# Value projection of a two-layer transformer by seven products of blocks in units of two token tiles

## The chip, the cores and the metric

The kernel runs on one core of one Trainium2 chip. A core has a matrix engine (TensorE, PE in the profile, with its weight loads as PEld), a vector engine (VectorE, DVE), a scalar engine (ScalarE, ACT), GpSimd (POOL) and SyncE (SP), whose queue issues this kernel's DMA transfers. The metric is the device time of one execution in microseconds (us); less is better. All data are float32.

## The reference

Two layers, each with attention and a feed-forward part side by side on the same normalised input, for 2 batches of 1024 tokens of 512 features and 16 heads of 32. Layer 0 has 2048 hidden units, layer 1 has 1408, ternary weights and scales.

```python
x = L0_attn_X                                   # (2, 1024, 512)
xn = _layernorm(x)
x = x + _L0_attn_ref(xn, Wq, Wk, Wv, Wo) + _L0_ffn_ref(xn, w_gate, w_up, w_down)
xn = _layernorm(x)
x = x + _L1_attn_ref(xn, ...) + _L1_ffn_ref(xn, ...)

# attention, both layers, up to the kind of rope
Q = X @ Wq.T; K = X @ Wk.T; V = X @ Wv.T
Qr, Kr = _rope(heads of Q), _rope(heads of K)
scores = einsum('bhqd,bhkd->bhqk', Qr, Kr) * DH ** (-0.5)       # causal
heads = einsum('bhqk,bhkd->bqhd', softmax(scores), heads of V)
return heads @ Wo.T

# feed-forward, layer 0 (layer 1: the same with scales on gate, up and down)
return einsum('bsh,dh->bsd', silu(x @ w_gate.T) * (x @ w_up.T), w_down)
```

The change concerns `V = X @ Wv.T`: 1024 tokens by 512 features in, 512 features out, once for each layer and batch.

## The kernel before

**Phases and steps.** A phase is one layer and batch; there are four, run one after the other. In each phase the heads go in four groups of four; in a group the queries go in four blocks of 256, and a step is one query block against 256 keys. A group has 10 steps, a phase 40, and `t0` is a phase's first step. A step issues scores (`sc`), scales them, masks the last of a block, takes maxima (`rmax`, `mtr`, which come back by DMA as `mb`), subtracts them, takes exponentials, sums these on GpSimd (`acc`) and, five steps after the scores (LAG = 5), multiplies them with the values on TensorE (`av`). So the first values of a phase, those of token tiles 0 and 1, are read at step t0 + 5, tiles 2 and 3 at t0 + 7, 4 and 5 from t0 + 10.

**What fills TensorE.** Beside attention's own matmuls, the class `Fill` hands TensorE the other work, a share in each step that spreads what is left evenly over the steps left in the phase. Its lists are: `main` (units of the hidden layer and what stands between phases: transposes, first projections), `downs` (rows of the down projection), `outs` (rows of the output projection), `qk` (units of queries and keys that are to be taken into main from a given step on) and, before the change, `values`. `choose` takes the next one by what its operands are waiting for; when the next main item isn't ready or is held, only downs and outs may pass it.

**Units.** The hidden layer's gate and up projections, and the queries and keys of groups 1 to 3, were already computed by seven products of 2x2 blocks (the Winograd form of Strassen's scheme): a `Unit` has four items, `first`, `second`, `third` and `fourth`, with two, two, two and one products, two PSUM banks held through it (`x` and `y`), copies of banks by ScalarE (`keep`), and sums of weight blocks that GpSimd makes while the unit before is in its third (`nxt.sums()`) and fourth item (`nxt.more_sums()`). The sums of the input blocks are made once a phase (`xs`, `ln_sums`, `ln_last_sum`). `decide`, called after each second item, puts the next unit of `qk` into main after the running unit's fourth if its step is due. There are 53 such hidden units and 12 of queries and keys.

**Values before.** `project_v(ph, t)` (line 812) makes the values of token tiles t and t + 4 for t = 0 to 3. It multiplies the first half of the features of tile t (2 matmuls into bank `ps_v`), keeps a copy (`vv`), multiplies the difference of the two tiles' first halves (`t1`) and the second half of tile t + 4 (4 matmuls into `ps_w`), adds the copy (VectorE, tile t + 4), and finishes tile t in `ps_v` with the second half (2 matmuls, then a copy by ScalarE). These are eight products of blocks: 8 matmuls with 128 tokens as the weights and 512 output features as the moving columns for each two tiles, 32 in a phase. They are issued as items of their own of cost 8, from steps t0 + 4, 4, 5, 5 on (phase 0: from step 0), and at the latest at t0 + 4, 4, 6, 6 (`queue_phase`, line 1354), but not between a unit's second and fourth item.

**The planner.** All instructions are recorded into `Schedule`, which simulates engines with durations of its own, then sorts them anew with due times (`again`, line 340) and emits them. So any change to the work can move instructions everywhere in the program. All of them carry the recorder's line, 265, in the profile; groups are told apart by the tiles' names.

**Buffers that the change touches.** `tmp`, tag `xs`, has two buffers of one tile of 128 x 512: raw input of the layer norm, and operands of `scale_down` (line 890), which multiplies the eleven row blocks of layer 1's down weights by their scales during phase 0 and stores them for the last two phases (`wds`). `wv` has one buffer, loaded anew for each phase after the last values of the phase before.

Of the kernel before, what the change touches and what calls it, by code (L numbers as in the profile page):

```python
# [11 lines left out]
F32 = mybir.dt.float32  # L12
AF = mybir.ActivationFunctionType
ALU = mybir.AluOpType
# [4 lines left out]
P = 128  # L19
# [4 lines left out]
QC = T // P  # L24
# [16 lines left out]
def ts(n, size):  # L41
    return slice(n * size, (n + 1) * size)
# [364 lines left out]
def two_layers(ctx: ExitStack, tc: tile.TileContext, x_in, attn_w, ffn_w, ffn_s, rope, out):  # L407
# [39 lines left out]
    def bank(name, shape=(P, TB), hold=False):  # L447
        nc.advance(nc.tensor.free)
        n = min((n for n in range(3) if not bank_held[n]), key=lambda n: (bank_free(n), bank_last[n].first.seq if bank_last[n] else 0))
        bank_held[n] = hold  # L450
        t = bank_last[n] = p_m.tile(list(shape), F32, tag=f"m{n}", name=name)
        if hold:
            bank_of[name] = n
        return t

    def let_go(name):
        bank_held[bank_of.pop(name)] = False
# [131 lines left out]
        nc.sync.dma_start(out=w[:, 2:4, :], in_=src[D // 2 :, :].rearrange("(c p) e -> p c e", p=P))  # L589

    class Unit:

# [44 lines left out]
        def product(self, bank, a, b, start=False):  # L639
            for c in range(2):  # L640
# [6 lines left out]
                    skip_group_check=True,  # L647
                )

        def scale(self):  # L650

            return None

        def needs(self, kind):

            if kind == "second":
                return [self.one, self.s12]
            if kind == "third":
                return [self.u, self.p5, self.s4]
            if kind == "fourth":  # L660
                return [self.p5]
            return []

        def first(self):
            self.begin()
            a, _ = self.weights()
            x0 = xnT[self.ph, 0]
            self.x = bank(f"ux{self.name}", hold=True)
            self.product(self.x, a[:, 0:2], x0[:, 0:2], start=True)
            one = self.one = keep(self.x, f"p1{self.name}")  # L670
            z = bank(f"uz{self.name}")
            self.product(z, a[:, 2:4], x0[:, 2:4], start=True)
            self.c11(z, one)

        def second(self):
            t1, t2, _ = xs[self.ph]
            self.product(self.x, self.s12[:, 1], t2)
            self.u = keep(self.x, f"u{self.name}")
            self.y = bank(f"uy{self.name}", hold=True)
            self.product(self.y, self.s12[:, 0], t1, start=True)  # L680
            self.p5 = keep(self.y, f"p5{self.name}", self.scale())

        def third(self, nxt):
            _, b = self.weights()
            x1 = xnT[self.ph, 1]
            self.product(self.x, b[:, 0:2], x1[:, 0:2])
            if nxt:
                nxt.sums()
            if self.scale() is None:
                nc.vector.tensor_tensor(self.p5, self.x, self.p5, ALU.add)  # L690
            else:
                nc.vector.scalar_tensor_tensor(self.p5, self.x, self.scale(), self.p5, ALU.mult, ALU.add)
            self.c22(self.p5)
            self.product(self.y, self.s4, x1[:, 2:4])
            let_go(f"uy{self.name}")
            self.c12(self.y, self.u)

        def fourth(self, nxt):
            _, b = self.weights()
            self.product(self.x, b[:, 2:4], xs[self.ph][2])  # L700
            let_go(f"ux{self.name}")
            if nxt:
                nxt.more_sums()
            self.c21(self.x)

    def keep(bank, name, scale=None):
        t = t5_p.tile([P, TB], F32, tag="t5", name=name)
        if scale is None:
            nc.scalar.copy(t, bank)
        else:  # L710
            nc.scalar.activation(t, bank, AF.Copy, scale=scale)
        return t
# [50 lines left out]
    class QueriesKeys(Unit):  # L763
        def __init__(self, ph, g, opens):

            self.ph, self.g, self.name, self.opens = ph, g, f"_qk{ph}_{g}", opens
            self.kind, self.part = "qk", g
# [4 lines left out]
        def begin(self):  # L772
            pass
# [2 lines left out]
            nc.vector.tensor_tensor(one, bank, one, ALU.add)  # L776
            rotated(self.ph, self.g, "q", 0, one)

        def c22(self, k1):
            rotated(self.ph, self.g, "k", 1, k1)  # L780

        def c12(self, bank, u):
# [24 lines left out]
    def load_wv(ph):  # L807
        layer, _ = phases[ph]
        wv[ph] = wv_p.tile([P, DC, D], F32, tag="wv", name=f"wv{ph}")
        nc.sync.dma_start(out=wv[ph], in_=attn_w[layer][2].rearrange("(c p) e -> p c e", p=P))  # L810

    def project_v(ph, t):


        x0, x1, t1 = xnT[ph, 0], xnT[ph, 1], xs[ph][0]
        cols = ts(t, P)

        def product(bank, a, c0, start):
            for c in range(2):
                nc.tensor.matmul(  # L820
                    bank,
                    a[:, c, cols],
                    wv[ph][:, c0 + c, :],
                    start=(start and c == 0),
                    stop=(c == 1),
                    skip_group_check=True,
                )

        ps0 = bank(f"ps_v{ph}_{t}", hold=True)
        product(ps0, x0[:, 0:2], 0, True)  # L830
        both = keep(ps0, f"vv{ph}_{t}")
        ps1 = bank(f"ps_w{ph}_{t}")
        product(ps1, t1, 0, True)
        product(ps1, x1[:, 2:4], 2, False)
        for n in (0, 4):
            v[ph, t + n] = xp.tile([P, D], F32, tag=f"v{t + n}", name=f"v{ph}_{t + n}")
        nc.vector.tensor_tensor(v[ph, t + 4], ps1, both, ALU.add)
        product(ps0, x0[:, 2:4], 2, False)
        let_go(f"ps_v{ph}_{t}")
        nc.scalar.copy(v[ph, t], ps0)  # L840
        if t == QC // 2 - 1 and ph + 1 < len(phases):
            load_wv(ph + 1)

    parts = {}

# [98 lines left out]
    class Hidden(Unit):  # L944
# [19 lines left out]
        def c11(self, bank, one):  # L964
            nc.vector.tensor_tensor(self.h[0], bank, one, ALU.add)

        def c22(self, up):
            self.up = up

        def c12(self, bank, u):  # L970
            nc.vector.tensor_tensor(self.h[1], bank, u, ALU.add)
# [235 lines left out]
    class Fill:  # L1207
# [2 lines left out]


        def __init__(self):
            self.timed, self.main, self.downs, self.outs, self.qk, self.values = [], [], [], [], [], []

            self.later = 0.0
            self.turn = False
            self.unit = None
# [15 lines left out]
            self.main[at:at] = items  # L1233

        def left(self, end):
            n = 8.0 * len(self.values) + sum(item[0] for item in self.main) + self.later
            n += sum(len(d[2]) for d in self.downs) + 14.0 * len(self.qk)
            return n + sum(1.0 for o in self.outs if o[0] < end)

# [39 lines left out]
                    return o  # L1279
            return None  # L1280

        def do_values(self):
            self.values.pop(0)[2]()
            self.turn = False
            return 8.0

        def do_output(self, o):
            self.outs.remove(o)
            output_alone(*o[1:])
# [9 lines left out]
        def choose(self, step):  # L1299

            main = self.main[0] if self.main else None
            v = self.values[0] if self.values and self.values[0][0] <= step else None
            if main and main[2] in ("third", "fourth"):
                v = None
            if v and v[1] <= step:
                return self.do_values, 8.0
            o = self.late_output(step)
            if o and self.wait([oT[o[1], o[2], o[3] // 2]]) <= 0.0:
                return (lambda: self.do_output(o)), 1.0
            full = main and main[2] == "first" and self.downs and self.downs[0][0] <= main[4] - 2  # L1310
            one = (lambda: self.do_main(step)), main[0] if main else 0.0
            full = full or (main and main[2] == "third" and getattr(main[3], "opens", 0) > step)
            if main and not full:
                needs = main[3].needs(main[2]) if isinstance(main[3], Unit) else main[3]() if main[3] else []
                main_wait = self.wait(needs, 0 if main[2] in ("third", "fourth") else 1)
                if main_wait <= SOON or not main[0]:
                    return one
            else:
                main_wait = float("inf")
            if self.ready_down():  # L1320
                _, p, ks, t = self.downs[0]
                if self.wait([hT[p, k, t // 4] for k in ks]) < main_wait or full or not main:
                    return (lambda: self.do_down(step)), 2.0
            if v:
                return self.do_values, 8.0
            if main and not full:
                return one
            return ((lambda: self.do_output(o)), 1.0) if o else None
# [25 lines left out]
    def queue_phase(ph):  # L1354
# [7 lines left out]
            for t in range(QC):  # L1362
                fill.outs.append((t0 + g * per_group + done_at(ph, g, t), ph, g, t))
        fill.outs.sort()
        for t in range(QC // 2):

            fill.values.append((t0 + (4, 4, 5, 5)[t] if ph else 0, t0 + (4, 4, 6, 6)[t], lambda t=t: project_v(ph, t)))
        if ph == 0:
            for k in range(HIDDEN[1]):
                fill.at(t0 + 4 + k, lambda k=k: scale_down(k))  # L1370
        if nxt:
            for t in range(QC):
                fill.at(t0 + per_phase - 22 + t, lambda t=t: load_raw(nxt, t))
# [217 lines left out]
```

## Time and profile before

| what | us |
| --- | --- |
| median of three runs | 1867.2 (1863.83 to 1868.71) |
| the profiled execution: time | 1868.41 |
| the profiled execution: span from its first to its last instruction | 1866.6 |
| value matmuls `ps_v`, busy | 60.9 |
| value matmuls `ps_w`, busy | 60.3 |
| hidden units' matmuls `ux`, `uy`, `uz`, busy (7 groups of 212) | 703.2 |
| down projection `d` from `hT`, busy | 401.0 |
| ScalarE copies `vv` and `v`, 16 each | 9.2 and 9.3 |
| VectorE adds into `v`, 16 | 11.0 |

The granted TensorE clock was 0.997 on the mean of the span. A row of the groups reads: engine, operation, what is written and read, shapes, count, then busy time and mean duration (ns) of one, then the engine's idle time before these instructions and what ended it. Matmul durations include a pipeline's length and overlap from one to the next; busy time counts an overlapped stretch once. "issue" is a wait for nothing that the profile shows.

### The profile page before, as it was taken

Reading aid. Unit: us, or ns where it says so; the run is one execution under the profiler, and the core shown is the slowest. Engines: PE = TensorE matmul, PEld = TensorE weight load, DVE = VectorE, ACT = ScalarE, POOL = GpSimd, SP = SyncE. Lnnn points to the kernel's source line nnn. Section 1 sums busy time; section 2 is a strip of 40 time slices with the busy share of each in tenths; the row PEclk is TensorE's granted clock in tenths of the full one; section 3 lists DMA queues with packets and bytes.
Section 4 is the critical chain, followed back from the end, with each engine's and each line's share of the span. In section 5 each row is a group of like instructions: output and inputs, shape, how many; then the busy total and the mean of one; then the engine's idle time right before and its main releaser. Section 6 shows DMA issues by size and latency. Waiting matters only on the chain.

```text
span 1866.6 us, 25444 instructions
## 1 busy us (share of the span) xinstructions
PE 1838.2 (98%) x9180; PEld 838.8 (45%) x9180; DVE 1408.2 (75%) x1958; ACT 1038.8 (56%) x1243; POOL 1179.8 (63%) x1124
## 2 busy tenths in 40 slices
PE   7999999999999999999999999999999999999997
PEld 3444444444444444444444444444444444444443
DVE  3577866758778577587587786978879887989787
ACT  3465554546557464445375645665665665666661
POOL 5575856756567355373356875878758766766664
PEclk9999999999999999999999999999999999999998
DMA  5544222222243222222223323222222312221111
GB/s 197 161 140 140 83 65 68 85 66 83 68 136 108 94 80 63 68 79 81 68 82 102 119 85 129 64 74 73 80 83 88 124 35 91 72 69 52 57 39 67
DMA packets 139726, 164.21 MB, mean 88 GB/s; under 512 B 13264, under 2 KB 93136, under 8 KB 139600
## 3 DMA queue, kind: packets, MB, share of 16 engines
q1 hardware_dynamic: 139600, 162.58, 27.5%
q8 instruction: 73, 1.20, 0.3%
q14 instruction: 53, 0.43, 0.1%
HBM read 134.23 MB, written 28.31 MB: 87 GB/s over the span
## 4 chain that ended last, share of the span: by engine, by line
PE 88%; DVE 5%; DMA 3%; POOL 2%; ACT 1%; issue 1%; SPq 0%; POOLq 0%; DVEq 0%; ACTq 0%
PE d L265 23%; PE ux L265 18%; PE uy L265 8%; PE av L265 8%; PE sc L265 8%; PE uz L265 4%; PE ux_qk L265 4%; PE ps_w L265 3%; PE ps_v L265 3%; DVE s L265 2%; PE uy_qk L265 2%; PE ps_k L265 2%; PE ps_o L265 1%; PE ps_q L265 1%; DMA mb<-md 1%
## 5 line engine op out<-in xcount | busy, mean ns | idle before, releaser
L265 DVE TENSOR_TENSOR s<-s,mb 128x1024 f32<-128x1024 f32 (+2 forms) x448 | 492.1, 1132 | 24.7 <-DMA mb<-md 24.7
L265 POOL TENSOR_TENSOR acc<-acc,s 128x512 f32<-128x512 f32 (+1 forms) x384 | 478.1, 1270 | 39.5 <-ACT s L265 38.0
L265 ACT ACTIVATE s<-s 128x1024 f32<-128x1024 f32 (+1 forms) x320 | 305.3, 971 | 182.0 <-DVE s L265 179.7
L265 DVE TRANSPOSE_TENSOR_REDUCE rmax<-s 128x32 f32<-128x1024 f32 (+1 forms) x320 | 350.9, 1118 | 72.5 <-POOL s L265 42.1
L265 PE MATMUL d<-wd,hT 128*128 128x512 f32 x864 | 401.0, 597 | 0.4 <-ACT xnT L265 0.2
L265 ACT ACTIVATE s<-sc 128x1024 f32<-128x1024 f32 (+1 forms) x320 | 282.9, 933 | 207.9 <-PE sc L265 204.0
L265 POOL TENSOR_TENSOR acc<-s 128x512 f32<-128x512 f32 (+1 forms) x128 | 153.6, 1214 | 235.4 <-PE av L265 173.2
L265 PEld LDWEIGHTS d<-wd,hT 128*128 128x128 f32 x864 | 162.8, 191 | 201.1 <-issue 187.3
L265 DVE TENSOR_TENSOR x<-d,x 128x512 f32<-128x512 f32 x224 | 151.7, 678 | 93.1 <-PE d L265 92.1
L265 ACT ACT_TABLE_LOAD x160 | 205.3, 1283 | 10.9 <-DVE s L265 8.1
L265 PE MATMUL av<-s,v 128*32 128x256 f32 (+1 forms) x2560 | 159.7, 365 | 3.0 <-ACT s L265 2.0
L265 PEld LDWEIGHTS av<-s,v 128*32 128x32 f32 x2560 | 66.9, 109 | 148.7 <-issue 105.0
L265 POOL TENSOR_SCALAR_AFFINE_SELECT s<-s 128x512 f32<-128x512 f32 x128 | 89.9, 716 | 66.6 <-ACT s L265 64.9
L265 POOL TENSOR_TENSOR hT<-p,hT 128x512 f32<-128x512 f32 x53 | 75.8, 1430 | 75.2 <-ACT hT L265 75.2
L265 PE MATMUL ux<-xs,wu 128*128 128x512 f32 x212 | 100.8, 598 | 3.1 <-DVE p L265 3.1
L265 PE MATMUL ux<-xnT,wu 128*128 128x512 f32 x212 | 101.5, 601 | 0.0
L265 PE MATMUL ux<-xs,ws 128*128 128x512 f32 x212 | 101.0, 599 | 0.0
L265 PE MATMUL ux<-xnT,wg 128*128 128x512 f32 x212 | 101.0, 599 | 0.0
L265 PE MATMUL uy<-xnT,ws 128*128 128x512 f32 x212 | 99.7, 593 | 0.0
L265 PE MATMUL uz<-xnT,wg 128*128 128x512 f32 x212 | 99.6, 592 | 0.0
L265 PE MATMUL uy<-xs,ws 128*128 128x512 f32 x212 | 99.6, 592 | 0.0
L265 PE MATMUL d<-wo,oT 128*128 128x512 f32 x192 | 99.3, 599 | 0.1
(158 smaller groups left out, 2412.7 us busy)
## 6 DMA issues: line engine op xcount, KB each, us to landing
mb<-md SPq DMA_DIRECT2D x64, 512.0 KB, 3.7
wg<-in_gate SPq DMA_DIRECT2D x54, 256.0 KB, 2.8
wd<-in_down SPq DMA_DIRECT2D x32, 256.0 KB, 3.0
xr<-xm SPq DMA_DIRECT2D x32, 256.0 KB, 3.1
wu<-in_up SPq DMA_DIRECT2D x28, 256.0 KB, 2.9
s12gu<-ws SPq DMA_DIRECT2D x26, 256.0 KB, 2.0
ws<-s12gu SPq DMA_DIRECT2D x26, 256.0 KB, 2.6
wd<-wds SPq DMA_DIRECT2D x22, 256.0 KB, 2.9
```

What stands on the lines that cost most here:

```text
L265: target(*[get(a) for a in args], **{k: get(a) for k, a in kwargs.items()})
```

## The change

- `project_v` goes, and a class `Values(Unit)` comes: two units a phase, `pair` 0 and 1. Pair 0 makes token tiles 0, 1, 4, 5, pair 1 makes 2, 3, 6, 7. Each has seven products of blocks. A product has four matmuls (two token tiles, two blocks of 128 features) with 128 tokens as weights and 256 output features as moving columns; the two tiles' results stand side by side in one bank, 256 columns each, and only the first matmul of the bank is flagged as a start.
- Sums of blocks of `wv` are made once a phase by GpSimd, on 128 x 512 elements each: s1, s2 (in the two `xs` buffers of `tmp`), s4 (a new buffer `wv4`), and A11 - A21 in place in `wv`. Both pairs use them.
- Values are written by halves of the features for two tiles at once: three VectorE adds and one ScalarE copy a unit, besides the three copies `keep`. The value tiles are now pairs, with the same total size.
- The values' list, its item `do_values` and its two steps go. The two units stand in `qk` with steps t0 + 3 and t0 + 4, and `begins` holds their first items until t0 + 4 and t0 + 5, in phase 0 too.
- `Unit.first`, `second`, `third`, `fourth` take their blocks from `first_blocks` and `blocks`; the add that ended `third` stands in each unit's `c22`; `needs` names the sums of inputs too.
- `scale_down(k)` moves from step 4 + k to step 9 + 3k/4 of phase 0.

```diff
     class Unit:
+        s4 = None
...
+        def blocks(self):
+            a, b = self.weights()
+            return (a[:, 0:2], a[:, 2:4], b[:, 0:2], b[:, 2:4]), (self.s12[:, 0], self.s12[:, 1]), self.s4
...
             if kind == "second":
-                return [self.one, self.s12]
+                return [self.one, *self.sums_in(), *xs[self.ph]]
             if kind == "third":
-                return [self.u, self.p5, self.s4]
+                return [self.u, self.p5, self.s4, xnT[self.ph, 1]]
...
-            if self.scale() is None:
-                nc.vector.tensor_tensor(self.p5, self.x, self.p5, ALU.add)
-            else:
-                nc.vector.scalar_tensor_tensor(self.p5, self.x, self.scale(), self.p5, ALU.mult, ALU.add)
-            self.c22(self.p5)
+            self.c22(self.x, self.p5)
...
-    def project_v(ph, t):
...
+    class Values(Unit):
+        HALF = D // 2
+        shared = {}
+
+        def __init__(self, ph, pair, begins):
+            self.ph, self.pair, self.name, self.begins = ph, pair, f"_v{ph}_{pair}", begins
+
+        def quarter(self, c, r):
+            return wv[self.ph][:, 2 * c : 2 * c + 2, r * self.HALF : (r + 1) * self.HALF]
+
+        def first_blocks(self):
+            return self.quarter(0, 0), self.quarter(1, 0)
+
+        def blocks(self):
+            s1, s2, s4 = self.shared[self.ph]
+            a = self.quarter(0, 0), self.quarter(1, 0), self.quarter(0, 1), self.quarter(1, 1)
+            return a, (s1, s2), s4
+
+        def sums(self):
+            if self.ph in self.shared:
+                return
+            a11, a21, a22 = self.quarter(0, 0), self.quarter(0, 1), self.quarter(1, 1)
+            s1, s2 = (tmp.tile([P, 2, self.HALF], F32, tag="xs", name=f"s{n}_v{self.ph}") for n in (1, 2))
+            s4 = ws_p.tile([P, 2, self.HALF], F32, tag="wv4", name=f"s4_v{self.ph}")
+            self.shared[self.ph] = s1, s2, s4
+            nc.gpsimd.tensor_tensor(s1, a21, a22, ALU.add)
+            nc.gpsimd.tensor_tensor(s2, s1, a11, ALU.subtract)
+
+        def more_sums(self):
+            s1, s2, self.s4 = self.shared[self.ph]
+            if self.pair == 0:
+                nc.gpsimd.tensor_tensor(self.s4, self.quarter(1, 0), s2, ALU.subtract)
+                a21 = self.quarter(0, 1)
+                nc.gpsimd.tensor_tensor(a21, self.quarter(0, 0), a21, ALU.subtract)
+
+        def product(self, bank, a, b, start=False):
+            for n in range(2):
+                for c in range(2):
+                    nc.tensor.matmul(
+                        bank[:, n * self.HALF : (n + 1) * self.HALF],
+                        b[:, c, ts(2 * self.pair + n, P)],
+                        a[:, c, :],
+                        start=(start and n == 0 and c == 0),
+                        stop=(c == 1),
+                        skip_group_check=True,
+                    )
+
+        def begin(self):
+            self.v = [xp.tile([P, 2, D], F32, tag=f"v{self.pair}{n}", name=f"v{self.ph}_{self.pair}{n}") for n in range(2)]
...
+        def c11(self, bank, one):
+            nc.vector.tensor_tensor(self.part(0, 0), self.pair_of(bank), self.pair_of(one), ALU.add)
+
+        def c22(self, bank, p5):
+            nc.vector.tensor_tensor(self.part(1, 1), self.pair_of(bank), self.pair_of(p5), ALU.add)
+
+        def c12(self, bank, u):
+            nc.vector.tensor_tensor(self.part(1, 0), self.pair_of(bank), self.pair_of(u), ALU.add)
+
+        def c21(self, bank):
+            nc.scalar.copy(self.part(0, 1), self.pair_of(bank))
...
             full = full or (main and main[2] == "third" and getattr(main[3], "opens", 0) > step)
+            full = full or (main and main[2] == "first" and getattr(main[3], "begins", 0) > step)
...
-        for t in range(QC // 2):
-            fill.values.append((t0 + (4, 4, 5, 5)[t] if ph else 0, t0 + (4, 4, 6, 6)[t], lambda t=t: project_v(ph, t)))
+        for pair in range(2):
+            begins = t0 + 4 + pair
+            fill.qk.append((begins - 1, Values(ph, pair, begins)))
+        fill.qk.sort(key=lambda x: x[0])
         if ph == 0:
             for k in range(HIDDEN[1]):
-                fill.at(t0 + 4 + k, lambda k=k: scale_down(k))
+                fill.at(t0 + 9 + 3 * k // 4, lambda k=k: scale_down(k))
```

More of the change, by code (lines that the diff above doesn't have):

```diff
@@ L665, in first, with sums_in @@
             self.begin()
-            a, _ = self.weights()
+            a11, a12 = self.first_blocks()
             x0 = xnT[self.ph, 0]
             self.x = bank(f"ux{self.name}", hold=True)
-            self.product(self.x, a[:, 0:2], x0[:, 0:2], start=True)
+            self.product(self.x, a11, x0[:, 0:2], start=True)
             one = self.one = keep(self.x, f"p1{self.name}")
             z = bank(f"uz{self.name}")
-            self.product(z, a[:, 2:4], x0[:, 2:4], start=True)
+            self.product(z, a12, x0[:, 2:4], start=True)
             self.c11(z, one)
+        def first_blocks(self):
+            a, _ = self.weights()
+            return a[:, 0:2], a[:, 2:4]
+        def sums_in(self):
+            return [self.s12]
         def second(self):
             t1, t2, _ = xs[self.ph]
-            self.product(self.x, self.s12[:, 1], t2)
+            _, (s1, s2), _ = self.blocks()
+            self.product(self.x, s2, t2)
             self.u = keep(self.x, f"u{self.name}")
             self.y = bank(f"uy{self.name}", hold=True)
-            self.product(self.y, self.s12[:, 0], t1, start=True)
+            self.product(self.y, s1, t1, start=True)
             self.p5 = keep(self.y, f"p5{self.name}", self.scale())
         def third(self, nxt):
-            _, b = self.weights()
+            (_, _, s3, _), _, s4 = self.blocks()
             x1 = xnT[self.ph, 1]
-            self.product(self.x, b[:, 0:2], x1[:, 0:2])
+            self.product(self.x, s3, x1[:, 0:2])
             if nxt:
                 nxt.sums()
-            if self.scale() is None:
-                nc.vector.tensor_tensor(self.p5, self.x, self.p5, ALU.add)
-            else:
-                nc.vector.scalar_tensor_tensor(self.p5, self.x, self.scale(), self.p5, ALU.mult, ALU.add)
-            self.c22(self.p5)
-            self.product(self.y, self.s4, x1[:, 2:4])
+            self.c22(self.x, self.p5)
+            self.product(self.y, s4, x1[:, 2:4])
             let_go(f"uy{self.name}")
@@ L698, in fourth @@
         def fourth(self, nxt):
-            _, b = self.weights()
-            self.product(self.x, b[:, 2:4], xs[self.ph][2])
+            (_, _, _, a22), _, _ = self.blocks()
+            self.product(self.x, a22, xs[self.ph][2])
             let_go(f"ux{self.name}")
@@ L777, in c11, with c22 @@
             rotated(self.ph, self.g, "q", 0, one)
-        def c22(self, k1):
+        def c22(self, bank, k1):
+            nc.vector.tensor_tensor(k1, bank, k1, ALU.add)
             rotated(self.ph, self.g, "k", 1, k1)
@@ L810, in load_wv, with first_blocks, sums_in, part @@
         nc.sync.dma_start(out=wv[ph], in_=attn_w[layer][2].rearrange("(c p) e -> p c e", p=P))
-    def project_v(ph, t):
[L815 to L842, printed above, removed]
+    class Values(Unit):
[5 more added lines that the diff above has]
+            return wv[self.ph][:, 2 * c : 2 * c + 2, r * self.HALF : (r + 1) * self.HALF]
+        def first_blocks(self):
+            return self.quarter(0, 0), self.quarter(1, 0)
[12 more added lines that the diff above has]
+            nc.gpsimd.tensor_tensor(s2, s1, a11, ALU.subtract)
+        def sums_in(self):
+            return list(self.shared[self.ph][:2])
+        def more_sums(self):
[17 more added lines that the diff above has]
+            self.v = [xp.tile([P, 2, D], F32, tag=f"v{self.pair}{n}", name=f"v{self.ph}_{self.pair}{n}") for n in range(2)]
+        def part(self, n, r):
+            return self.v[n][:, :, r * self.HALF : (r + 1) * self.HALF]
+        def pair_of(self, t):
+            return t.rearrange("p (n e) -> p n e", n=2)
+        def c11(self, bank, one):
[6 more added lines that the diff above has]
+            nc.scalar.copy(self.part(0, 1), self.pair_of(bank))
+            for n in range(2):
+                for i in range(2):
+                    v[self.ph, 4 * n + 2 * self.pair + i] = self.v[n][:, i, :]
+            if self.pair == 1 and self.ph + 1 < len(phases):
+                load_wv(self.ph + 1)
@@ L965, in c11, with c22 @@
             nc.vector.tensor_tensor(self.h[0], bank, one, ALU.add)
-        def c22(self, up):
+        def c22(self, bank, up):
             self.up = up
+            if self.scale() is None:
+                nc.vector.tensor_tensor(up, bank, up, ALU.add)
+            else:
+                nc.vector.scalar_tensor_tensor(up, bank, self.scale(), up, ALU.mult, ALU.add)
         def c12(self, bank, u):
@@ L1212, in __init__ @@
         def __init__(self):
-            self.timed, self.main, self.downs, self.outs, self.qk, self.values = [], [], [], [], [], []
+            self.timed, self.main, self.downs, self.outs, self.qk = [], [], [], [], []
             self.later = 0.0
@@ L1235, in left @@
         def left(self, end):
-            n = 8.0 * len(self.values) + sum(item[0] for item in self.main) + self.later
+            n = sum(item[0] for item in self.main) + self.later
             n += sum(len(d[2]) for d in self.downs) + 14.0 * len(self.qk)
@@ L1280, in late_output @@
             return None
[L1282 to L1285, printed above, removed]
         def do_output(self, o):
@@ L1301, in choose @@
             main = self.main[0] if self.main else None
[L1302 to L1306, printed above, removed]
             o = self.late_output(step)
@@ L1323, in choose @@
                     return (lambda: self.do_down(step)), 2.0
-            if v:
-                return self.do_values, 8.0
             if main and not full:
```

## The prediction

> **What bounds the kernel now.** I read the page's engine totals first, then the chain of waits that ended last.
>
> ```profile
> span 1866.6 us, 25444 instructions
> PE 1838.2 (98%) x9180; PEld 838.8 (45%) x9180; DVE 1408.2 (75%) x1958; ACT 1038.8 (56%) x1243; POOL 1179.8 (63%) x1124
> PE 88%; DVE 5%; DMA 3%; POOL 2%; ACT 1%; issue 1%; SPq 0%; POOLq 0%; DVEq 0%; ACTq 0%
> ```
>
> TensorE is busy for 98% and is 88% of the chain: the kernel lasts as long as TensorE's stream of matmuls, and 1866.6 - 1838.2 = 28.4 us is all that waiting costs. A busy matmul engine need not be a matmul engine at its peak, so next I asked for the matmuls that the change touches, each shape apart, and then for the same stretch in the chain told in order of time.
>
> ```profile
> L265 PE MATMUL ps_v<-wv,xnT 128*128 128x512 f32 x128 | 60.9, 601 | 0.0
> L265 PE MATMUL ps_w<-wv,xs 128*128 128x512 f32 x64 | 30.2, 594 | 0.3 <-DVE p_qk L265 0.3
> L265 PE MATMUL ps_w<-wv,xnT 128*128 128x512 f32 x64 | 30.1, 592 | 0.0
> ...
> 598.52 3.43 PE ps_w L265 x8
> 601.96 1.72 PE ps_v L265 x4
> ```
>
> The program issues 32 matmuls of values per phase, 128 in all, and the trace lists 256: each float32 matmul is two records, each with its own weight load. The mean durations (592 to 601 ns) overlap; the spacing is what counts: 3.43 us / 8 = 429 ns a record. So the values take 256 x 0.429 = 109.8 us of TensorE, with 0.3 us of waiting: 6% of the span, all of it on the chain.
>
> Third, the stages where values run, and the last stage (columns: length, then busy time and count for PE, PEld, DVE, ACT, POOL; clock; DMA).
>
> ```profile
> 556.10:620.00 63.90, 63.90 (x318) 29.32 (x314) 48.74 (x73) 39.84 (x49) 41.35 (x35) 1.00 0.27 85
> 1082.00:1140.00 58.00, 57.75 (x302) 25.86 (x302) 44.75 (x60) 32.23 (x39) 32.29 (x33) 1.00 0.13 44
> 1480.00:1540.00 60.00, 58.80 (x326) 26.57 (x321) 53.88 (x76) 37.40 (x47) 43.41 (x40) 1.00 0.17 54
> 1560.00:1840.00 280.00, 274.28 (x1545) 123.92 (x1545) 245.97 (x317) 175.93 (x196) 192.19 (x165) 0.98 0.19 59
> ```
>
> TensorE is the limit in all four; VectorE comes nearer from stage to stage: 76%, 77%, 90%, 88%.
>
> **Part 1: the products, on the path.** Removed: 256 records of 512 columns. Added: 7 products x 4 matmuls x 2 units x 4 phases = 224 matmuls of 256 columns, 448 records. No full 128-row, 128-column matmul of 256 columns stands in the trace, so its spacing is bounded by its neighbours:
>
> ```profile
> 508.61 0.60 PE L265 MATMUL tr<-ident,xr 128*128 128x128 f32 x4
> 509.05 1.02 PE L265 MATMUL ps_o<-wo,oT 128*128 128x512 f32 x2
> ...
> L265 PEld LDWEIGHTS tr<-ident,xr 128*128 128x128 f32 x96 | 11.4, 141 | 10.6 <-issue 7.7 <-ACT xnT L265 1.1 <-DVE s L265 0.8
> ...
> 506.89 0.21 PEld L265 LDWEIGHTS sc<-q_1T,k_3T 32*128 32x128 f32 x4
> ...
> 507.11 0.20 PEld L265 LDWEIGHTS sc<-q_1T,k_3T 32*128 32x128 f32 x4
> ```
>
> Four transposes of 128 columns take 509.05 - 508.61 = 0.44 us, 110 ns each, although each has a load of 141 ns. In the scores, with 256 columns, each of four row groups gets a new load every 507.11 - 506.89 = 0.22 us. At the 429 ns row's rate a 256-column record takes 429 / 2 = 214.5 ns; on the line through 110 ns at 128 columns and 429 ns at 512 it takes 110 + 128 x (319 / 384) = 216 ns. That is 448 x 0.2145 = 96.1 us or 448 x 0.216 = 96.8 us, a gain of 13.7 or 13.0 us. I take 13.7, by the row that is the same operation, and keep 13.0. A load of these tiles takes 190 ns, so under 214.5 ns it still has cover, but with only 24 ns to spare where 239 were before.
>
> The Trainium skill speaks against this. "TensorE: Matmul & The Clock Gate", under "Measured speedup vs the span model", says that a weight load overlaps running matmuls only if its row group differs; under "LDWEIGHTS (loading the stationary operand)" it gives columns / 1.2 ns, 107 ns for 128. By these each of the 192 added records would add 107 ns to the stream, an estimate of 20.5 us, and the sum would end at 6.8 us slower instead of 13.7 faster. Here the rows disagree with it: full-array records with a 190 ns load follow each other at 429 ns, with nothing left over for a load.
>
> **Part 2: new work beside the path.** GpSimd gets four sums of 512 elements per phase (s1, s2, s4, and A11 - A21 in place): 16 in all. VectorE gets three adds per unit where it had one per token tile: 24 for 16, with halves of two tiles as output. ScalarE has as many copies as before, four per unit against two per tile.
>
> ```profile
> L265 POOL TENSOR_TENSOR wr<-wr,ds x11: 1264/1268/2257, 49.0 to 137.4; 128x512 f32<-128x512 f32 x11
> L265 DVE TENSOR_TENSOR v<-ps_w,vv 128x512 f32<-128x512 f32 x16 | 11.0, 686 | 16.6 <-PE ps_w L265 16.0 <-ACT s L265 0.7
> ```
>
> GpSimd: 16 x 1.27 = 20.3 us, 5.1 per phase. VectorE: 8 x 0.686 = 5.5 us. Both fall under TensorE's stream, so I cost them at nothing. The four sums run while the unit before and the first product run, and the planner takes rows of the down projection when s1 and s2 are late. Without that cover, 5.1 us a phase is the price.
>
> **Part 3: the chain inside a unit.** A values unit now has the hidden units' waits: its second product goes into the bank that ScalarE is copying, its fourth into one that VectorE is reading. From the list of waits:
>
> ```profile
> PE ux L265 <- DVE p L265: 3.1, 4, 1.4
> ...
> PE uy_qk L265 <- DVE x L265: 0.7, 1, 0.7
> ```
>
> 53 hidden and 12 query/key units wait 3.8 us together, 0.06 each; eight more cost 0.5 us. From below the 0.3 us at ps_w goes away; from above every one has the longest, 8 x 1.4 = 11 us. I take 0.5: such waits struck in 5 cases of 65.
>
> **Part 4: order and gates.** A values unit is queued when a unit's second product runs at step t0 + 2 or later, and its first product is held until t0 + 4. What is queued behind it is all the main work; only down and output rows may pass. Following the code along the timeline, in phases 1 and 2 the second product that queues it is that of a hidden unit at t0 + 3, and it starts on time. In phase 3 it is the query/key unit's at t0 + 2 (1481.10 us): at t0 + 3, where the hidden unit's first product now fills in, the gate is closed and no down rows are there. That step becomes nearly bare, and one bare step shows what it costs:
>
> ```profile
> 1519.33 1.07 PE L265 MATMUL av<-s,v 128*32 128x256 f32 x16 [0.79 <-DVE oT L265]
> ```
>
> 0.8 us, once; from 0 (earlier steps have run ahead) to 4 x 0.8 = 3.2. The first weighted sum of a phase now waits for a whole two-tile value; its last writer is a ScalarE copy, as before, and costs what it cost, within 0.6 us a phase. In phase 0 the values go from steps 0 to 7 to steps 4 to 6 and hidden work takes their place: nothing, TensorE is full there. The eleven products with down_s go five steps later, with 22 loads and 11 stores past what is queued on SP and 1.27 us each on GpSimd: nothing, their rows are first read at 988 us. The add that moves into c22 and the longer lists of needs issue nothing.
>
> **Sum.** The profiled execution took 1868.41 us (span 1866.6, 1.8 around it). 1868.4 - 13.7 + 0.5 + 0.8 = 1856.0; it lay 1.2 above the median of the runs shown, so I forecast **1854.8 us**, 0.7% faster. Below: the planner lays the whole program out anew, and if about 6 of the 28.4 us of waiting went, 1849. Above, within this case: 13.0 for 13.7, 3.2 for 0.8 and some 3 us of chain waits, 1861. Own range 1849 to 1861.
>
> **Rivals.**
> (a) *Part of it is given back in layer 1.* VectorE is at 88 to 90% of phase 3, and from 1809 to 1828 us the chain runs through it, not TensorE. If attention sets the pace there and in phase 2, their share, 2 x 3.4 = 6.9 us, is lost: 1862, and up to 1868 with new waits. For it: that chain. Against: TensorE is at 98% even from 1480 to 1540 and from 1560 to 1840 us.
> (b) *Slower: the loads come out from under the shorter streams.* Break-even is 109.8 / 448 = 245 ns a record. If 190 ns of load keep no cover, a record takes 404 ns: 448 x 0.404 - 109.8 = 71 us, 1938. If only half of the load shows, 310 ns, 29 us: 1896. Against: the transposes.
> (c) *Slower: sums and gate starve TensorE at each phase's start.* Uncovered, 5.1 us of sums and 0.8 of a bare step, four times: 24 - 13.7 = 10, 1877. From 3.4 us a phase it eats the gain. For it: three links in a row inside two steps. Against: the down rows that fill such holes, which are missing in phase 3 alone.
> (d) *It doesn't do what it says:* the planner's new order elsewhere costs as much as the products bring, no change, 1867.
>
> **Chances.** Forecast 0.68; (a) 0.14; (b) 0.05; (c) 0.08; (d) 0.05. This measurement tells about 0.3%, 5.6 us, from no change: faster is under 1861.6, slower over 1872.8. Faster: 0.68 and a third of (a), 0.73. Same: the rest of (a) and most of (d), 0.14. Slower: 0.13. The range reaches from 1849 to 1868, over (a) and (d).
>
> **What would show it.** 448 value records 214 to 216 ns apart, TensorE busy some 13 us less, 16 more GpSimd and 8 more VectorE operations; waits of the values units under 1 us in all; a bare step at about 1485 us. Records at 245 ns or more would show (b), gaps before the units' second products (c), gaps before weighted sums after 1480 us (a).

## The result and the profile after

The changed kernel takes 1854.97 us (median of 6 runs, 1853.96 to 1860.38) against 1867.24 us of the kernel before in the same comparison: a ratio of 0.9942, 95% interval 0.9927 to 0.9956. The forecast was 1854.8 us. The profiled execution took 1856.87 us, 11.5 less than that of before.

The page's totals, to be held against those of before:

```profile
span 1855.1 us, 25877 instructions
PE 1823.7 (98%) x9372; PEld 874.5 (47%) x9372; DVE 1423.0 (77%) x1961; ACT 1029.7 (56%) x1234; POOL 1200.4 (65%) x1140
PE 89%; DVE 5%; DMA 2%; POOL 1%; issue 1%; ACT 1%; SPq 0%; ACTq 0%; POOLq 0%; DVEq 0%
```

TensorE is busy 14.5 us less with 192 records more, GpSimd 20.6 us more with 16 operations more, and TensorE is still what the chain runs through. Two of the six groups of value matmuls (the other four, of 64 records each, have no wait), a group of their weight loads (PEld), and two pieces of the chain in order of time (start, length, what):

```profile
L265 PE MATMUL ux_v<-wv,xnT 128*128 128x256 f32 x128 | 31.0, 385 | 0.0
L265 PE MATMUL ux_v<-wv,xs 128*128 128x256 f32 x64 | 15.3, 382 | 1.0 <-DVE v L265 0.9
...
L265 PEld LDWEIGHTS ux_v<-wv,xnT 128*128 128x128 f32 x128 | 23.7, 190 | 6.8 <-issue 3.1 <-DVE x L265 0.7
...
1513.62 1.73 PE ux_v L265 x8
1515.35 1.73 PE uy_v L265 x8
```

Eight records in 1.73 us are 216 ns each, half of the 429 of before, and each has a weight load of 190 ns (the second number of the PEld row). TensorE waited 1.0 us in all inside the values units.

Where the 11.5 us of the profiled executions come from is worked out from the trace: every matmul record's time from its start to the next one's start, less the idle time before the next, summed by kind.

```
us                                   before     after     change
value matmuls (256 / 448 records)     112.0      99.3     -12.7
attention's matmuls (5696)            346.6     345.9      -0.7
all other matmuls (3227)             1379.0    1377.9      -1.1
idle between matmuls                   15.5      19.0      +3.4
before the first, after the last       13.5      13.0      -0.5
span                                 1866.6    1855.1     -11.5
```

The value matmuls brought 12.7 us, and 3.4 us net were given back as waiting. These are some of TensorE's waits after the change (us in total, count, longest):

```profile
PE tr L265 <- ACT xn L265: 9.6, 3, 8.6
PE av L265 <- POOL acc L265: 6.5, 3, 3.1
...
PE ux_v L265 <- DVE v L265: 0.9, 1, 0.9
```

The wait for `acc`, GpSimd's sums of exponentials, was 2.9 us before, 2.6 of it in the kernel's last 40 us. What is new lies at the start of phase 3. TensorE's timeline there (start, length, instructions, and idle time before in brackets):

```profile
1480.11 1.15 PE L265 MATMUL sc<-q_1T,k_0T 32*128 32x256 f32 x16
1481.18 1.98 PE L265 MATMUL ux_qk<-xs,wk 128*128 128x512 f32 x4
...
1483.21 1.07 PE L265 MATMUL av<-s,v 128*32 128x256 f32 x16
1484.21 1.15 PE L265 MATMUL sc<-q_1T,k_0T 32*128 32x256 f32 x16
...
1504.38 0.86 PE L265 MATMUL av<-s,v 128*32 128x256 f32 x16
1506.58 0.63 PE L265 MATMUL av<-acc,ones 128*32 128x256 f32 x4 [1.34 <-POOL acc L265]
1509.26 0.77 PE L265 MATMUL av<-acc,ones 128*32 128x256 f32 x4 [2.05 <-POOL acc L265]
1509.96 2.09 PE L265 MATMUL sc<-q_1T,k_0T 32*128 32x256 f32 x16
```

From one score group to the next at 1480.11 and 1484.21 us there are 4.1 us with only one product of a unit, the last, in them: the bare step at t0 + 3 that the gate of the values units makes (a step holds its scores, then the fill, then the weighted values of five steps before). Two steps on, in step t0 + 5, TensorE waits 1.34 + 2.05 us for `acc`. In between, from 1487 to 1499 us, the chain leaves TensorE and runs for the most part through GpSimd, which makes `acc` and the rotated queries and keys; pieces of it in order of time:

```profile
1487.39 1.63 POOL acc L265
1489.02 1.23 POOL q_1T L265
1490.25 1.41 POOL k_1T L265
1491.67 1.42 POOL acc L265
```

The scores that follow the waits take 2.09 us where they took 1.15. The reason for that stands in the table by stages (length, busy of PE, PEld, DVE, ACT, POOL, clock, DMA):

```profile
1500.00:1509.50 9.50, 6.10 (x54) 4.25 (x56) 8.86 (x13) 5.56 (x7) 7.97 (x9) 1.00 0.00 0
1509.50:1513.00 3.50, 3.50 (x22) 1.74 (x19) 2.32 (x8) 0.83 (x1) 2.25 (x4) 0.52 0.00 0
```

After the waits the granted clock is a half for 3.4 us, which costs another 1.7. It is not the only such stretch: near the kernel's end the clock is halved for 10.2 us from 1829.7 us before the change and for 6.8 us from 1820.2 us after it. Counted with those, matmuls ran at half clock for 7.4 us before and 7.2 us after, so over the whole kernel the halved clock costs about the same. That the stretch at the end is shorter can't be put down to the change: the other profiles have 6.8 us there without the change, and 3.4, 6.8 or 10.2 with it, in this kernel and its variants below.

### The profile page after: what moved, and what is told of

Its sections match the earlier page's. It is cut to its first block, busy times and chain, and to the rows that moved or that the text cites. A ratio compares the mean times of both kernels' runs of the same rounds, so it can differ in the third digit from the quotient of the medians.

```text
span 1855.1 us, 25877 instructions
## 1 busy us (share of the span) xinstructions
PE 1823.7 (98%) x9372; PEld 874.5 (47%) x9372; DVE 1423.0 (77%) x1961; ACT 1029.7 (56%) x1234; POOL 1200.4 (65%) x1140
## 4 chain that ended last, share of the span: by engine, by line
PE 89%; DVE 5%; DMA 2%; POOL 1%; issue 1%; ACT 1%; SPq 0%; ACTq 0%; POOLq 0%; DVEq 0%
PE d L265 23%; PE ux L265 18%; PE uy L265 9%; PE av L265 9%; PE sc L265 8%; PE ux_qk L265 5%; PE uz L265 4%; DVE s L265 3%; PE uy_qk L265 2%; PE ux_v L265 2%; PE ps_k L265 2%; PE ps_q L265 1%; PE ps_o L265 1%; POOL acc L265 1%; PE uz_qk L265 1%; PE uy_v L265 1%
## 5 line engine op out<-in xcount | busy, mean ns | idle before, releaser
L265 DVE TENSOR_TENSOR s<-s,mb 128x1024 f32<-128x1024 f32 (+2 forms) x448 | 503.9, 1154 | 21.7 <-DMA mb<-md 21.5
L265 POOL TENSOR_SCALAR_AFFINE_SELECT s<-s 128x512 f32<-128x512 f32 x128 | 98.6, 787 | 54.3 <-ACT s L265 52.7
L265 PE MATMUL d<-wo,oT 128*128 128x512 f32 x202 | 104.5, 599 | 0.3 <-DVE x L265 0.3
```

The costliest lines, as they stand in the source:

```text
L265: target(*[get(a) for a in args], **{k: get(a) for k, a in kwargs.items()})
```

## The experiments

Each difference is taken to the runs that its text names; the kernel before had medians of 1868.06, 1866.97 and 1866.54 us in the three sets of runs. The changed kernel itself, run again in the second set:

> The changed kernel unedited, on the chip of the next three, as their mark: 1855 us, 12 us under the kernel before.

1857.01 us, ratio 0.9948 (0.9935 to 0.9960). So it stands 10 to 12 us under the kernel before, and its waits for `acc` in phase 3 came again with 1.34 and 2.05 us.

**Short streams alone.** The kernel before with each value matmul in two halves:

```diff
-            for c in range(2):
-                nc.tensor.matmul(bank, a[:, c, cols], wv[ph][:, c0 + c, :], ...)
+            for n in range(2):
+                for c in range(2):
+                    nc.tensor.matmul(bank[:, ts(n, D // 2)], a[:, c, cols], wv[ph][:, c0 + c, ts(n, D // 2)], ...)
```

> The kernel before with its eight products, each matmul of 512 output columns cut into two of 256 in one bank: the shape of the change without its saving. Theory (the gain is the shorter stream of products alone): 512 records 215.5 ns apart take 110.3 us where 256 records at 429 ns took 109.8, so 0.5 us more, and with a newly laid plan 1864 to 1871 us. Rival (short streams lay the weight loads bare): at 245 ns a record 15.6 us more, 1883 us or above.

1865.79 us, ratio 0.9991 (0.9982 to 0.9999). Pieces of its chain, to be held against 3.43 us for eight records of 512 in the kernel before:

```profile
599.09 3.45 PE ps_w L265 x16
602.54 1.73 PE ps_v L265 x8
```

Twice as many weight loads cost 0.02 us in 3.43. The rival in which the loads come to light is gone, and with it the thought that the shape alone could have brought or taken more than about 3 us.

**The product put back.** The eighth product in its new shape, everything else of the change kept:

```diff
             self.product(z, a12, x0[:, 2:4], start=True)
+            if isinstance(self, Values):              # second kernel: and self.ph >= 2
+                self.product(z, a12, x0[:, 2:4], start=True)
```

> The changed kernel in which each values unit makes its second product of blocks (bank uz) twice, the second time over the first: eight products of 256 columns, everything else of the change kept. Theory: 8 units x 8 records x 215.5 ns = 13.8 us more than the changed kernel, 1855 + 13.8 = 1869 us, all of the gain gone (1865 to 1872). Rival (attention sets the pace in layer 1, so TensorE's saving there is lost): only the 6.9 us of phases 0 and 1 show, 1862 us.

1868.64 us, ratio to the kernel before 1.0006 (0.9997 to 1.0015): the gain is gone. Against the changed kernel's two medians it is 11.6 to 13.7 us, against its profile the value matmuls rose by 13.2. The waits for `acc` at the start of phase 3 shrank to 0.24 and 0.53 us here, so part of the added work took the place of waiting.

> The same doubled product in phases 2 and 3 alone (layer 1). Theory: 4 units x 8 records x 215.5 ns = 6.9 us more than the changed kernel, 1862 us (1859 to 1865). Rival (attention sets the pace in layer 1): the extra products fall into waits that are there anyhow, 1855 to 1857 us.

1858.82 us, 2 to 4 us over the changed kernel where 6.9 were expected, and more than the rival's 0 to 2. By the same account of start to start, its value matmuls rose by 6.3 us against the changed kernel's profile, and its idle time fell by 3.9: with the longer units the waits for `acc` at that place shrank to 0.24 and 0.53 us, and no halved clock follows them.

```profile
1502.62 0.62 PE L265 MATMUL av<-acc,ones 128*32 128x256 f32 x4 [0.24 <-POOL acc L265]
```

So the number missed because a second thing moved, and the experiment had to be made where that thing isn't (below).

**More sums.** GpSimd's four sums made three times over:

```diff
-            nc.gpsimd.tensor_tensor(s1, a21, a22, ALU.add)
-            nc.gpsimd.tensor_tensor(s2, s1, a11, ALU.subtract)
+            for _ in range(3):
+                nc.gpsimd.tensor_tensor(s1, a21, a22, ALU.add)
+                nc.gpsimd.tensor_tensor(s2, s1, a11, ALU.subtract)
...
-                nc.gpsimd.tensor_tensor(self.s4, self.quarter(1, 0), s2, ALU.subtract)
-                nc.gpsimd.tensor_tensor(a21, self.quarter(0, 0), a21, ALU.subtract)
+                for _ in range(3):
+                    nc.gpsimd.tensor_tensor(self.s4, self.quarter(1, 0), s2, ALU.subtract)
+                    nc.gpsimd.tensor_tensor(a21, self.quarter(0, 0), a21, ALU.subtract)
```

> The changed kernel with each of the four sums of weight blocks made three times over: 12 instead of 4 GpSimd operations of 1.27 us a phase, 32 more in all, 40.7 us of GpSimd. Theory (the sums lie wholly beside TensorE): 1855 us, within 3 us. Rival (late sums starve TensorE at each phase's start): up to 10.2 us more in each phase, 1865 to 1896 us.

1865.36 us, 8 to 10 over the changed kernel: the theory missed. Its waits are not spread over the phases, as the rival had it, but stand in phase 3:

```profile
1502.69 1.77 PE L265 MATMUL av<-acc,ones 128*32 128x256 f32 x6 [5.32 <-POOL acc L265]
```

The trace shows why there: the last three of the repeated sums run on GpSimd between 1483.7 and 1492.8 us, and behind them come 11.0 us of `acc` for which TensorE waits. Are the change's own sums the cause of the waits for `acc` in the changed kernel, or the bare step? Two kernels tell these apart.

**The bare step filled.** Phase 3's values units are queued one step later, so that a hidden unit comes before them:

```diff
-            fill.qk.append((begins - 1, Values(ph, pair, begins)))
+            fill.qk.append((begins - 1 + (ph == 3), Values(ph, pair, begins)))
```

> The changed kernel with the values units of phase 3 queued one step later, so that a hidden unit runs at t0 + 3 in place of the bare step. Theory (the bare step starves attention two steps on, and TensorE then waits 3.4 us for acc): that wait falls under 1 us, 2 to 3.5 us faster than the changed kernel, about 1852 us. Rival (GpSimd is behind there because of the added sums): the wait stays, 1855 us.

1850.17 us, ratio 0.9916 (0.9901 to 0.9931), 6.8 under the changed kernel of the same runs, about twice what the theory gave; again in the third set:

> The version with phase 3's values units one step later, unedited, as mark for the next three: 1850 us, 17 under the kernel before.

1851.18 us, 0.9919 (0.9907 to 0.9932). The same stretch in the first of these two profiles:

```profile
1478.85 1.15 PE L265 MATMUL sc<-q_1T,k_0T 32*128 32x256 f32 x16
1479.92 1.98 PE L265 MATMUL ux_qk<-xs,wk 128*128 128x512 f32 x4
...
1481.85 1.88 PE L265 MATMUL ux<-xnT,wg 128*128 128x512 f32 x4
1483.57 1.88 PE L265 MATMUL uz<-xnT,wg 128*128 128x512 f32 x4
1485.38 1.07 PE L265 MATMUL av<-s,v 128*32 128x256 f32 x16
1486.38 1.15 PE L265 MATMUL sc<-q_1T,k_0T 32*128 32x256 f32 x16
...
1506.15 1.99 PE L265 MATMUL ux_v<-wv,xnT 128*128 128x256 f32 x8 [0.66 <-ACT u_v L265]
```

The step holds a hidden unit's first two products and lasts 7.5 us; no weighted sum waits for `acc` in the window, in either profile. Between 1478 and 1512 us GpSimd was busy 31.7 of 34 us in the changed kernel, 27.4 here and 30.0 in the second profile. Of the 7.9 us by which the first profile's span is shorter than the changed kernel's, 4.0 are idle time and 2.2 attention's matmuls, some 1.5 of these from less halved clock. The second profile is only 3.4 us shorter: 2.9 of idle time and 2.2 of attention's matmuls went, but the other matmuls took 2.8 more. So the waits explain 3 to 4 us, the halved clock behind them up to 1.7, and the rest of the 6.8 is not traced. This version beats both kernels.

**The sums left out where the waits are.**

```diff
+            if self.ph == 3:
+                self.shared[self.ph] = a22, a11, a21
+                return
```

(`more_sums` leaves out phase 3 likewise.)

> The changed kernel in whose phase 3 the four sums of weight blocks are left out and plain blocks take their place, so that phase's values are others than the reference's; 5.1 us of GpSimd less. Theory (bare step): the wait of 3.4 us for acc stays, 1855 us within 2. Rival (GpSimd behind because of the added sums): it goes, about 1852 us.

1858.00 us, ratio 0.9950 (0.9938 to 0.9963): 1.0 over the theory's range and over the changed kernel of the same runs, so no faster, and the waits for `acc` are 1.34 and 2.04 us at the same place. The trace of the changed kernel shows why the sums don't matter: phase 3's run from 1456.2 to 1461.3 us, some 45 us before the waits (first and last start in us behind the durations):

```profile
L265 POOL TENSOR_TENSOR s_v<-wv,s_v x4: 1273/1276/1277, 53.9 to 1460.0; 128x512 f32<-128x512 f32 x4
```

The sums of the change do not make the waits, and filling the bare step takes them away. The bare step isn't enough alone: in both kernels above with a product put back the step is just as bare (4.1 us), and the longer units behind it leave waits of 0.24 and 0.53 us.

**Tests without the bare step.** On the version with phase 3 queued later:

> That version with each of the four sums made three times over, 40.7 us of GpSimd more. Theory (the sums are covered unless a bare step has let attention fall behind): 1850 us, within 3 us. Rival (the sums have a price of their own, as the 8 us of the first such run would say): 1856 us or above.

1855.34 us, 4.2 more than that version's 1851.18: between the theory's 3 and the rival's 6. About half of what three-fold sums cost with the bare step is there without it. In its profile a wait for `acc` of 1.37 us and 3.4 us of half clock follow at 1506 us, the same place; one of the repeated sums, 1.8 us long, runs at 1498.2 us in front of that `acc`. So GpSimd operations have a price where the planner puts them just ahead of `acc`; phase 3's share of the change's own 20.3 us, left out above, showed none. The other phases were not tried.

> That version with the doubled product in phases 2 and 3 alone. Theory (the first such run showed 2 to 4 us in place of 6.9 because the longer units also closed the wait of 3.4 us for acc): here that wait isn't there, so the whole 6.9 us, 1857 us (1854 to 1860). Rival (attention sets the pace in layer 1): 1850 to 1853 us.

1858.54 us, 7.4 more than 1851.18: the 6.9 of the theory. Its value matmuls take 6.7 us more than in that version's profile of the same set, and its idle time fell by only 0.6.

> That version with the doubled product in all eight values units. Theory: 13.8 us more than it, 1864 us (1861 to 1867). Rival (TensorE's saving is lost where attention sets the pace): 1857 us.

1868.38 us, 17.2 more than 1851.18, 3.4 over the theory and above its range. Its profiled execution ran the first 363 us at a granted clock of 0.95 and isn't read for this, so what the 3.4 us are stays open. It ends where the changed kernel with the same doubled product ended, at 1868.64 us: that one had only waits of 0.24 and 0.53 us for `acc` left, so queueing phase 3 later had little to gain there.

**One edit alone.** The kernel before with the eleven products with down_s moved:

```diff
-                fill.at(t0 + 4 + k, lambda k=k: scale_down(k))
+                fill.at(t0 + 9 + 3 * k // 4, lambda k=k: scale_down(k))
```

> The kernel before with one part of the change alone: the eleven products with down_s from step 9 + 3k/4 in place of 4 + k. Theory: nothing waits for them until 988 us, so the kernel before's time, 1864 to 1870 us. Rival: they share GpSimd and the transfers with other work of the steps they come into, a few us slower.

1866.81 us, ratio 1.0000 (0.9991 to 1.0010): no difference.

## Why the prediction was right, point by point

- **The bound.** That TensorE's stream sets the time, in layer 1 too, is shown by the product put back: 1868.64 us with it in all phases, and 7.4 us for 6.9 in phases 2 and 3 once no other wait could hide it. Rival (a), attention as the limit there, falls. The waits before weighted sums after 1480 us, its sign, did come, but they were the bare step's.
- **The products, -13.7.** The mechanism and nearly the size were right. The spacing was 215 to 216 ns instead of 214.5, nearer to the 216 that the line through the neighbours' rows gave; 448 x 0.2155 = 96.5 us, a gain of 13.3 by spacing and 12.7 by the account of start to start. Rival (b) falls with the 3.45 us for sixteen records.
- **A rule weighed.** The Trainium skill, "TensorE: Matmul & The Clock Gate", ties the overlap of a weight load with running matmuls to another row group; the sentence stands under "The mechanism", just before the section that the prediction names. Here loads of the whole array, 190 ns each where the formula that the prediction took from the page gives 107, pass under 216 ns streams of the whole array, so it doesn't hold for this form; the estimate of 20.5 us from it did not come.
- **New work beside the path, 0.** Sixteen GpSimd operations at 1.27 us and 24 VectorE adds at 0.67 us came as counted. Leaving out phase 3's sums brought nothing. That more of them would be free as well, as the later theory had it, was wrong: three times the sums cost 4 us without a bare step, 8 to 10 with it. Rival (c) had that price in each phase and put the waits at the units' second products; they came in phase 3 alone, at the weighted sums. It fell as a forecast, but the gate, half of its mechanism, did act.
- **Waits inside a unit, +0.5.** 1.0 us, the one of 0.9 at a fourth product behind VectorE.
- **The bare step, +0.8.** The place was right to the step, the size was not: 3.4 us of waiting, and 1.7 us of halved clock behind it, 5 us in place of 0.8; filling the step gained 6.8. The row I priced it by, 0.79 us behind VectorE, shows a wait right after one bare step. Here the wait came two steps later and for another engine: the whole held unit ran in the next step, and the step after that had only two products in front of its weighted values. The sum that these need, of a query block's first step, is issued in that very step, and GpSimd hadn't finished it. That GpSimd was late because the bare step gave it too little time fits the chain above, but no run shows how much each of these steps adds.
- **The sum.** Terms of -13.7, +0.5 and +0.8 gave -12.4; the profiled executions differ by 11.5. The bare step was under-sized by some 4 us; the larger part of that was offset by rows that I had set at nothing: 1.1 us of other matmuls, 0.9 of it by less halved clock (10.2 us near the kernel's end before, 6.8 after), and 0.7 of attention's, 0.5 at the two ends, and waits elsewhere that the new plan no longer has. So the closeness of 1854.8 to 1855.0 is partly luck: the sum's main term holds by itself, the small ones do not.

## What to carry to other kernels

When a stream of matmuls is the bound, fewer columns are worth what the spacing of the records says, even if each stream becomes as short as its weight load; read the spacing, not the mean duration. Then look for where the new work is held back: a gate that left one step bare cost 5 us two steps later, in a wait for another engine and the halved clock behind it, and one line that queued the unit a step later brought 6.8 us where the algorithm had brought 10 to 12.

## What was not expected of the hardware

The clock was halved for 3.4 us behind two waits of 1.34 and 2.05 us that had 0.63 us of matmuls between them. The Trainium skill, "TensorE: Matmul & The Clock Gate", "HAM oscillation — how this bites in real kernels", warns of idle gaps above about 3.4 us; here neither gap was that long. The stretches of half clock in this case's profiles last 3.41 us, or two or three times that, if the program doesn't end sooner. So take, in the traces of the 14 runs after their first 100 us, windows of 3.41 us that line up with these stretches, and add up TensorE's idle time in each. The 26 windows at full clock behind which the clock was halved held 1.8 to 3.4 us of it (2.4 in the changed kernel's phase 3); of some 7000 others at full clock none held more than 1.9. Here, then, idle time added up over several gaps, and a little over half of a window was enough.
